# Six TensorE transposes per loop step replaced: a block-wise load with VectorE transposes, and score rows spread through DRAM

## The chip, the cores and the metric

The kernel runs on one core of one Trainium2 chip. The metric is device time in microseconds (us) of a whole execution, as the median of several executions. Engines are named as the profile names them: PE is the matrix engine TensorE, DVE is VectorE, ACT is ScalarE, and SP is the engine whose queue issues all the DMAs here.

## The reference, cut to what matters

Two graph layers over 128 batches of 128 nodes with 512 features. The inputs are `x` (128, 128, 512), `adj` (128, 128, 128) and a mask of ones.

```python
# layer 0, per batch: h = relu(layernorm(x))
Xw = h @ Wv + bv
sj, si = Xw @ aw[:d, 0], Xw @ aw[d:, 0]
e = leaky_relu(sj[:, None, :] + si[:, :, None] + ab[0], 0.2)
alpha = A * exp(e)
transition = alpha / (sum(alpha, axis=-1, keepdims=True) + 1e-12)
for k in range(3):
    H = H + Xk @ Wk[k] + bk[k];  Xk = transition @ Xk
x = x + relu(H)
# layer 1: h = relu(layernorm(x)); q, k = split(h @ Wqk); v = h @ Wv
agg = adj @ (k * mask)
w = inv_scale * mask * sum(q * agg, axis=-1)
x = x + softmax(w, axis=1)[:, :, None] * v
```

Three things in it need something turned by 90 degrees. `sj` is a column with one value per node (partition), and every partition needs all 128 values as a row. The softmax over `w` needs the same for its maximum and its sum. The product `adj @ k` needs A^T: the kernel hands PE the left operand of a product in transposed form.

## The kernel before

The kernel works on pairs of batches (`G` = 2), so it has 64 loop steps. In each step it runs layer 0 of pair p and layer 1 of pair p-1. The scores come from h by two dot products per batch on DVE, with folded weights `u_bc`. The parts that the change and the argument touch:

```python
    def spread(dst, col):                 # a column to a row on every partition
        nc.tensor.transpose(dst, col.to_broadcast([P, P]), ident)

    def norm0(p):
        ...
        h = H[p] = norm_relu(xg[p], "h", front)
        HV[p] = by_blocks(h)              # h to DRAM and back, block-wise
        s = S[p] = small.tile([P, G, 2], FP, name="s")
        for j in range(G):
            for a in range(2):            # the four score sums, DVE
                nc.vector.scalar_tensor_tensor(junk, h[:, j, :], 1.0, u_bc[:, a, :], ...,
                                               accum_out=s[:, j, a:a + 1])

    def attention(p):
        for j in range(G):
            spread(pz[:, j, :], s[:, j, 0:1])                          # PE, 2 transposes
        ... z = pz + s1 + cz, leaky step, exp, times A, row sums, t ...
        for j in range(G):
            nc.tensor.transpose(pa[:, j, :], a[:, j, :], ident)        # PE, 2 transposes: A^T
        ... ACT copies pa into AT[p] with the mask as scale

    def finish(p, yv, w):
        for j in range(G):
            spread(pw[:, j, :], w[:, 0, j:j + 1])                      # PE, 2 transposes
        ... maximum (DVE), exponential (ACT), sum, x = x + weight * v, store

    # the loop: strassen0 is 7 layer-0 products; its steps run between them
    steps = (lambda: (begin(n), attention(n), end()), lambda: t_transposed(n))
    strassen0(p, steps); propagate(p + 1)
    H2[p] = norm_relu(X1[p], ...); hv2 = by_blocks(H2[p])
    yv = strassen1(p - 1); w = aggregate(p - 1, yv)   # layer 1
    prepare0(p + 1); ...; norm0(p + 2)
```

`end()` calls `finish` for the pair whose weights are ready. `strassen0` and `strassen1` accumulate their products in three PSUM banks each, and DVE must read a bank before PE may write the next sum of products into it. `t_transposed` transposes the transition matrix on PE, and ACT copies it out.

## Time and profile before

| of the kernel before | value | how to read it |
|---|---|---|
| time | 2432.89 us (2430.91 to 2434.4, 6 runs) | |
| PE busy | 2382.0 us, 98% of the span | PE has hardly a gap |
| DVE busy / ACT busy | 74% / 27% | both have room on average |
| mean granted PE clock | 0.995 | near full speed; the changed kernel below shows it falling after a wait |
| loop period | 36.70 us | from two equal points of the chain of waits |
| DMAs that write pieces under 64 bytes to DRAM | none | no record stands for the new 4-byte writes |

The prediction shows the lines that carry this. A "period" is the distance in time between two equal points of the chain in successive loop steps. With PE at 98%, the sum of PE's pieces in one period is what a change has to lower.

### The profile page before, as it was taken

The numbers are of one execution on the slowest core, as the hardware profiler recorded it, in microseconds if no ns is written. First come the engines' busy times: TensorE is split into PE (matmuls) and PEld (weight loads), VectorE is DVE, ScalarE is ACT, GpSimd is POOL, SyncE is SP. The second block draws the span as 40 slices with busy tenths as digits, with TensorE's granted clock in tenths as the row PEclk, the third lists the DMA queues.
The fourth block names the chain that finished last, engine by engine and source line by source line (L and its number), as shares of the span: only waits on it lengthen the run. The fifth ranks groups of instructions, "written<-read, shape, count | busy, mean of one in ns | idle before, by whom it ended". The sixth has DMA issues, their size and how long they took to land.

```text
span 2429.0 us, 27235 instructions
## 1 busy us (share of the span) xinstructions
PE 2382.0 (98%) x9289; PEld 1694.0 (70%) x9289; DVE 1791.6 (74%) x4776; ACT 647.6 (27%) x1549; POOL 0.7 (0%) x6
## 2 busy tenths in 40 slices
PE   4999999999999999999999999999999999999997
PEld 3676776776776776776776766766767767767764
DVE  6677777777777777777777777777777777777764
ACT  2223223222222222222222222222232232222221
POOL 0000000000000000000000000000000000000000
PEclk9999999999999999999999999999999999999998
DMA  6233232332332332331332332332332323323311
GB/s 202 72 100 92 80 100 87 85 100 81 91 100 75 97 100 67 105 100 63 109 99 64 108 94 70 102 95 75 100 93 79 100 88 84 100 83 89 96 52 52
DMA packets 236939, 220.49 MB, mean 91 GB/s; under 512 B 14336, under 2 KB 170112, under 8 KB 236800
## 3 DMA queue, kind: packets, MB, share of 16 engines
q1 hardware_dynamic: 236800, 218.75, 31.0%
q8 instruction: 73, 1.20, 0.2%
q14 instruction: 66, 0.54, 0.1%
HBM read 118.03 MB, written 100.66 MB: 90 GB/s over the span
## 4 chain that ended last, share of the span: by engine, by line
PE 97%; DVE 2%; DMA 1%; ACT 0%; issue 0%; SPq 0%; DVEq 0%; ACTq 0%
PE pm L340 79%; PE pt L319 9%; PE pt L411 4%; PE pt L307 1%; PE pt L138 1%; PE pt L303 1%; PE pm L205 1%; PE pt L292 1%; DMA wv_sb<-in_L_gnn_Wv_dram 0%; DVE st L218 0%; DVE junk L249 0%; DVE junk L147 0%; DVE x L378 0%; DVE x L265 0%; DMA hv<-hd 0%
## 5 line engine op out<-in xcount | busy, mean ns | idle before, releaser
L340 PE MATMUL pm<-t,sx 128*128 128x256 f32 x2304 | 518.2, 379 | 0.0
L340 PEld LDWEIGHTS pm<-t,sx 128*128 128x128 f32 x2304 | 432.8, 190 | 56.2
L340 PE MATMUL pm<-b,x 128*128 128x256 f32 x1536 | 362.8, 379 | 0.0
L340 PE MATMUL pm<-f,sx 128*128 128x512 f32 x768 | 344.9, 598 | 0.3 <-DVE s L392 0.2
L340 PEld LDWEIGHTS pm<-b,x 128*128 128x128 f32 x1536 | 282.3, 190 | 60.1 <-issue 30.1
L321 ACT COPY x<-pt 128x512 f32<-128x512 f32 x256 | 148.9, 582 | 500.1 <-PE pt L319 500.1
L340 PEld LDWEIGHTS pm<-f,sx 128*128 128x128 f32 x768 | 141.5, 190 | 194.0 <-issue 154.5
L340 PE MATMUL pm<-e,x 128*128 128x512 f32 x512 | 242.5, 596 | 6.6 <-DVE x L265 6.6
L319 PE MATMUL pt<-tt,h 128*128 128x256 f32 x1024 | 234.5, 383 | 0.9 <-ACT tt L308 0.9
L319 PEld LDWEIGHTS pt<-tt,h 128*128 128x128 f32 x1024 | 196.4, 192 | 28.7 <-ACT tt L308 1.5
L249 DVE SCALAR_TENSOR_TENSOR junk<-h,u_bc 128x512 f32<-128x512 f32 x256 | 176.4, 689 | 8.5 <-ACT h L233 1.8
L340 PE MATMUL pm<-b,sx 128*128 128x256 f32 x768 | 176.2, 379 | 0.0
L340 PE MATMUL pm<-t,x 128*128 128x256 f32 x768 | 176.2, 379 | 0.0
L233 ACT ACTIVATE h<-x,rs 128x512 f32<-128x512 f32 x128 | 97.2, 807 | 289.9 <-PE pt L411 278.3
L265 DVE STREAM_TRANSPOSE x<-hv 128x512 f32<-128x512 f32 x256 | 166.4, 688 | 4.7 <-DMA hv<-hd 3.8
L340 PEld LDWEIGHTS pm<-e,x 128*128 128x128 f32 x512 | 97.7, 191 | 103.1 <-issue 92.2
L340 PEld LDWEIGHTS pm<-b,sx 128*128 128x128 f32 x768 | 145.9, 190 | 19.8
L340 PEld LDWEIGHTS pm<-t,x 128*128 128x128 f32 x768 | 145.9, 190 | 19.8
L400 DVE TENSOR_TENSOR yv<-pm,s 128x512 f32<-128x512 f32 x64 | 44.2, 691 | 128.7 <-PE pm L340 128.7
L233 ACT ACTIVATE h<-xg,rs 128x512 f32<-128x512 f32 x128 | 97.3, 807 | 118.7 <-DVE rs L230 118.7
L411 PE MATMUL pt<-h,aT 128*128 128x512 f32 x256 | 120.5, 592 | 0.5 <-ACT h L233 0.5
L340 PE MATMUL pm<-f,x 128*128 128x512 f32 x256 | 120.3, 592 | 0.0
(102 smaller groups left out, 2508.3 us busy)
## 6 DMA issues: line engine op xcount, KB each, us to landing
hd<-h SPq DMA_DIRECT2D x128, 512.0 KB, 3.3
hv<-hd SPq DMA_DIRECT2D x512, 128.0 KB, 3.3
xg<-in_x_dram SPq DMA_DIRECT2D x64, 512.0 KB, 3.6
out_dram<-x SPq DMA_DIRECT2D x64, 512.0 KB, 3.1
ag<-in_adj_dram SPq DMA_DIRECT2D x64, 128.0 KB, 3.0
b<-in_L_gnn_Wk_dram SPq DMA_DIRECT2D x8, 256.0 KB, 3.4
w<-in_L_gnn_Wqk_dram SPq DMA_DIRECT2D x8, 256.0 KB, 5.3
wv_sb<-in_L_gnn_Wv_dram SPq DMA_DIRECT2D x1, 1024.0 KB, 7.6
```

Source lines behind the costliest of these rows:

```text
L138: nc.tensor.transpose(dst, col.to_broadcast([P, P]), ident)
L205: nc.tensor.matmul(pm[c], wt[0][:, c * P:(c + 1) * P], wt[1], start=(o == 0), stop=(o == DC - 1))
L233: nc.scalar.activation(h[:, j, :], src[:, j, :], AF.Relu, bias=rs[:, 1, j:j + 1], scale=rs[:, 0, j:j + 1])
L249: nc.vector.scalar_tensor_tensor(junk, h[:, j, :], 1.0, u_bc[:, a, :], op0=OP.mult, op1=OP.mult, accum_out=s[:, j, a:a + 1])
L265: nc.vector.transpose(dst[:, j].rearrange("p f (n b) -> p f n b", n=Q), hv[:, j].rearrange("p n (f a) -> p f n a", f=Q))
L292: nc.tensor.transpose(pa[:, j, :], a[:, j, :], ident)
L303: nc.tensor.transpose(pt[:, j, :], t[:, j, :], ident)
L319: nc.tensor.matmul(pt[:, c].rearrange("p k n -> p (k n)"), h[:, j, at:at + P], tt[:, j].rearrange("p k n -> p (k n)"), start=True, stop=True)
L321: nc.scalar.copy(X[p][:, 1:3, j, kh].rearrange("p k c n -> p c k n"), pt)
L340: nc.tensor.matmul(bank[:, :r.shape[-1]], left[i][:, k, c * P:(c + 1) * P], r, start=(first and at == 0), stop=(at == len(chunks) - 1), sk ...
L400: nc.vector.tensor_add(o[0][1], b, s[:, 0])
L411: nc.tensor.matmul(pa, at[:, j, :], h2[:, j, :], start=True, stop=True)
```

## The change

The intent is to take six small PE transposes out of each loop step. A^T is loaded a second time, as 32x32 blocks already in their transposed places (`agb`), and DVE transposes inside the blocks. The score column and the weight column are written to DRAM as 4-byte pieces and read back as one 1 KB row broadcast to all 128 partitions. To give those round trips time, the score sums move forward, between the layer-1 products. The core of the diff:

```diff
+        agb[p] = loads.tile([P, G, Q, S32], FP, name="agb", bufs=2)
+        v = adj[s].rearrange("g (q b) (c i) -> c b (g q) i", b=S32, i=S32)
+        for c in range(Q):
+            nc.sync.dma_start(agb[p][c * S32:(c + 1) * S32].rearrange("p g q i -> p (g q) i"), v[c])
...
+    def spread_pair(col, name, by_dma):
+        if by_dma:
+            d = dram.tile([G, N], FP, name=f"{name}d")
+            nc.sync.dma_start(d.rearrange("g n -> n g"), col)
+            dst = front.tile([P, G, N], FP, name=name, bufs=1)
+            nc.sync.dma_start(dst.rearrange("p g n -> p (g n)"), bcast(d, 0, G * N))
+            return dst
...                                        # attention
-        for j in range(G):
-            spread(pz[:, j, :], s[:, j, 0:1])
...
-        for j in range(G):
-            nc.tensor.transpose(pa[:, j, :], a[:, j, :], ident)
+        nc.vector.transpose(AT[p].rearrange("p g n -> p (g n)"),
+                            agb.pop(p).rearrange("p g q i -> p (g q i)"))
...                                        # strassen1, before its last two product groups
+        if ahead < NP:
+            score_sums(ahead)              # the four sums, then spread_pair(s, "pz", p > 0)
...                                        # the loop
-                steps = (lambda: (begin(n), attention(n), end()), lambda: t_transposed(n))
+                steps = (lambda: (begin(n), attention(n)), lambda: (t_transposed(n), end()))
...
-            ends.append((p - 1, yv, w))
+            ends.append((p - 1, yv, w, spread_pair(w[:, 0], "pw", p < NP)))
```

The set-up code was also reordered (the projection weights are loaded in four pieces, and norm0 of the next pair moves forward). The first scores and the last weights keep their PE transposes.

More of the change, by code (lines that the diff above doesn't have):

```diff
@@ L64, in bcast @@
         return bass.AP(tensor=ap.tensor, offset=ap.offset + offset, ap=[[0, P], [1, n]])
-    xg, ag = {}, {}
+    xg, ag, agb = {}, {}, {}
     def load(p):
@@ L83, with spread @@
     nc.sync.dma_start(aw_bc.rearrange("p a d -> p (a d)"), bcast(aw, 0, 2 * D))
-    wv0_sb = upool.tile([P, DC, D], FP, name="wv0_sb")
-    nc.sync.dma_start(wv0_sb, wv0.rearrange("(c p) o -> p c o", p=P))
+    ident = const.tile([P, P], FP, name="ident")
+    make_identity(nc, ident)
+    eps = const.tile([P, 1], FP, name="eps")
+    nc.vector.memset(eps, EPS)
+    def spread(dst, col):
+        nc.tensor.transpose(dst, col.to_broadcast([P, P]), ident)
+    u_bc = const.tile([P, 2, D], FP, name="u_bc")
+    ucol = setup.tile([P, 2, DC], FP, name="ucol")
+    ccol = setup.tile([P, 2], FP, name="ccol")
+    for c in range(DC):
+        wv0_sb = upool.tile([P, D], FP, name="wv0_sb", bufs=2)
+        nc.sync.dma_start(wv0_sb, wv0[c * P:(c + 1) * P])
+        for a in range(2):
+            junk = front.tile([P, D], FP, name="junk", bufs=1)
+            nc.vector.scalar_tensor_tensor(junk, wv0_sb, 1.0, aw_bc[:, a, :], op0=OP.mult,
+                                           op1=OP.mult, accum_out=ucol[:, a, c:c + 1])
     bv_bc = upool.tile([P, D], FP, name="bv_bc")
@@ L118 @@
         if k:
-            bk_bc.append(setup.tile([P, D], FP, name=f"bk{k}_bc"))
+            bk_bc.append(upool.tile([P, D], FP, name=f"bk{k}_bc"))
         nc.sync.dma_start(bk_bc[k], bcast(bk, k * D, D))
@@ L129 @@
             rows(e[kh, nh][:, :, 1, :], wv1[:, nh * HD:(nh + 1) * HD], kh)
-    ident = const.tile([P, P], FP, name="ident")
-    make_identity(nc, ident)
-    eps = const.tile([P, 1], FP, name="eps")
-    nc.vector.memset(eps, EPS)
-    def spread(dst, col):
-        nc.tensor.transpose(dst, col.to_broadcast([P, P]), ident)
-    u_bc = const.tile([P, 2, D], FP, name="u_bc")
-    ucol = setup.tile([P, 2, DC], FP, name="ucol")
-    ccol = setup.tile([P, 2], FP, name="ccol")
     for a in range(2):
-        for c in range(DC):
-            junk = front.tile([P, D], FP, name="junk", bufs=1)
-            nc.vector.scalar_tensor_tensor(junk, wv0_sb[:, c, :], 1.0, aw_bc[:, a, :],
-                                           op0=OP.mult, op1=OP.mult, accum_out=ucol[:, a, c:c + 1])
         pu = ps_t.tile([P, DC, P], FP, name="pt")
@@ L235, in norm_relu @@
         return h
-    H, HV, S, X, SX, AT, T, TT, X1, H2, X2, SX2 = ({} for _ in range(12))
+    H, HV, S, PZ, X, SX, AT, T, TT, X1, H2, X2, SX2 = ({} for _ in range(13))
     def norm0(p):
@@ L244, in norm0, with score_sums @@
         HV[p] = by_blocks(h)
+    def score_sums(p):
+        h = H[p]
         s = S[p] = small.tile([P, G, 2], FP, name="s")
@@ L250, in norm0 @@
                                                op1=OP.mult, accum_out=s[:, j, a:a + 1])
+        PZ[p] = spread_pair(s[:, :, 0], "pz", p > 0)
     def by_blocks(h):
@@ L266, in transposed, with attention @@
                                 hv[:, j].rearrange("p n (f a) -> p f n a", f=Q))
-    def attention(p):
-        a, s = ag.pop(p), S.pop(p)
+    def spread_pair(col, name, by_dma):
[5 more added lines that the diff above has]
+            return dst
         pz = ps_t.tile([P, DC, P], FP, name="pt")
         for j in range(G):
-            spread(pz[:, j, :], s[:, j, 0:1])
+            spread(pz[:, j, :], col[:, j:j + 1])
+        return pz[:, :G]
+    def attention(p):
+        a, s, pz = ag.pop(p), S.pop(p), PZ.pop(p)
         z = front.tile([P, G, N], FP, name="z", bufs=1)
@@ L277, in attention @@
         nc.vector.scalar_tensor_tensor(z, z, 0.2, z, op0=OP.mult, op1=OP.max)
-        ex = front.tile([P, G, N], FP, name="ex")
+        ex = z
         nc.scalar.activation(ex, z, AF.Exp)
@@ L288, in attention @@
             nc.vector.tensor_scalar(t[:, j, :], ex[:, j, :], d[:, 1, j:j + 1], None, op0=OP.mult)
-        pa = ps_t.tile([P, DC, P], FP, name="pt")
-        for j in range(G):
-            nc.tensor.transpose(pa[:, j, :], a[:, j, :], ident)
         AT[p] = front.tile([P, G, N], FP, name="aT", bufs=3)
+        nc.vector.transpose(AT[p].rearrange("p g n -> p (g n)"),
+                            agb.pop(p).rearrange("p g q i -> p (g q i)"))
         for j in range(G):
             b = p * G + j
-            nc.scalar.activation(AT[p][:, j, :], pa[:, j, :], AF.Copy, scale=maskT[:, b:b + 1])
+            nc.scalar.activation(AT[p][:, j, :], AT[p][:, j, :], AF.Copy, scale=maskT[:, b:b + 1])
     def t_transposed(p):
@@ L379, in strassen0, with strassen1 @@
                                            op0=OP.max, op1=OP.add)
-    def strassen1(p):
+    def strassen1(p, ahead):
         product = products(SX2.pop(p), R1)
@@ L418, in aggregate, with finish @@
         return w
-    def finish(p, yv, w):
-        pw = ps_t.tile([P, DC, P], FP, name="pt")
-        for j in range(G):
-            spread(pw[:, j, :], w[:, 0, j:j + 1])
-        nc.vector.tensor_reduce(w[:, 1], pw[:, :G, :], AX.X, OP.max, negate=True)
+    def finish(p, yv, w, pw):
+        nc.vector.tensor_reduce(w[:, 1], pw, AX.X, OP.max, negate=True)
         for j in range(G):
@@ L445 @@
     norm0(0)
+    score_sums(0)
     begin(0)
@@ L451 @@
     norm0(1)
+    score_sums(1)
     R1 = None
@@ L462 @@
                 n = p + 1
-                steps = (lambda: (begin(n), attention(n), end()), lambda: t_transposed(n))
+                steps = (lambda: (begin(n), attention(n)), lambda: (t_transposed(n), end()))
             else:
-                steps = (end, lambda: None)
+                steps = (lambda: None, end)
             strassen0(p, steps)
@@ L478 @@
             hv2 = by_blocks(H2[p])
+        if p + 2 < NP:
+            norm0(p + 2)
         if p > 0:
-            yv = strassen1(p - 1)
+            yv = strassen1(p - 1, p + 2)
+        elif p + 2 < NP:
+            score_sums(p + 2)
+        if p > 0:
             w = aggregate(p - 1, yv)
@@ L491 @@
             SX2[p] = left_sums(a, late["p"], "sx2", [1, HD])
-        if p + 2 < NP:
-            norm0(p + 2)
     end()
```

## The prediction

> **What bounds the kernel now.** I read, in this order: the summary, the chain that ended last, the same chain inside one step of the loop, the busy time of that step, then the timeline around the operations that the change moves, and last the start and the end. The kernel does 64 pairs of batches; I call the repeating stretch between two equal points of the chain a period.
>
> The chain is TensorE work (PE) nearly from end to end; inside a period (columns: start us, length us, what) it has no piece of another engine:
>
> ```profile
> PE 97%; DVE 2%; DMA 1%; ACT 0%; issue 0%; SPq 0%; DVEq 0%; ACTq 0%
> ...
> 1225.46 5.18 PE pm L340 x24
> 1230.64 0.22 PE pt L138 x2
> 1230.86 0.22 PE pt L292 x2
> 1231.08 0.22 PE pt L138 x2
> 1231.30 5.18 PE pm L340 x24
> 1236.48 0.22 PE pt L303 x2
> ...
> 1262.16 5.18 PE pm L340 x24
> 1267.34 0.22 PE pt L138 x2
> ```
>
> The six transposes that the change removes are the three 0.22 us rows between the 24-record products: two for the score rows (L138), two for the adjacency (L292), two for the layer-1 weights (L138). The period is 1267.34 - 1230.64 = 36.70 us. The busy table of one period (window, its length, then PE, PEld, DVE, ACT, POOL, clock, DMA share, GB/s) says PE is never idle, VectorE (DVE) has 9 us free and the DMA engines 70%:
>
> ```profile
> 1225.50:1262.20 36.70, 36.70 (x145) 26.22 (x144) 27.59 (x74) 10.02 (x25) 0.00 (x0) 1.00 0.30 90
> ```
>
> A busy PE alone would not prove a limit, but the chain's pieces add up: 18.12 us of layer-0 products (84 records at 0.216), 3.45 propagation, 12.08 layer-1 products, 1.72 aggregation, 0.22 + 0.44 for the transition matrix, 0.66 for the six transposes: 36.7.
>
> **What the Trainium skill says.** "TensorE: Matmul & The Clock Gate", Part 4 (PE-mode transpose), gives about 275 ns for a 128x128 transpose in one kernel. The trace agrees on the record (mean 274 to 278 ns) but in the chain two take 0.22 us: records overlap, and what a transpose costs a full PE is 0.11 us. "VectorE: DVE Perf Modes", The three transpose paths, says DVE transposes 32x32 blocks, not a 128x128 tile; hence the block-wise load. Here a 128x512 block transpose (L265) takes 688 ns. "DMA: Bandwidth & Descriptors", Rules for kernel authors, says a DMA that reads what another wrote must be issued only after the first one's completion; the same page's Anatomy of one DMA puts the fixed cost near 2.0 us. So the spread through DRAM costs two latencies in a row. The trace agrees on both: times to landing (last column, us), and the wait of the DMA queue (total, times, longest):
>
> ```profile
> hd<-h SPq DMA_DIRECT2D x128, 512.0 KB, 3.3
> hv<-hd SPq DMA_DIRECT2D x512, 128.0 KB, 3.3
> ...
> e<-in_L_gnn_Wv_dram SPq DMA_DIRECT2D x16, 64.0 KB, 2.0
> ...
> SPq L259 <- DMA hd<-h: 125.5, 66, 2.4
> ```
>
> **Part 1: PE work removed.** In steady state six transposes a period, 6 x 0.11 = 0.66 us; the period should become 36.04 us. The order of the built kernel shows PE otherwise unchanged within a period. Scores and adjacency of pairs 2 to 63 and weights of pairs 0 to 61 lie under a full PE: 62 x 0.66 = 40.9 us. Pairs 0 and 1 are in the start, where PE idles, and the last weights keep their PE transposes.
>
> **Part 2: DVE and ACT.** Added: one 128x256 block transpose, about 0.4 us (half of L265's 688 ns plus overhead, an estimate). Cheaper: z read from SBUF instead of PSUM; z (401 ns each, L276) should approach the SBUF form of L288 (280 ns), saving 0.24, and the maximum (414 ns) a little. Net about zero on DVE's 27.6 us. ACT scales the adjacency from SBUF as it did from PSUM (364 ns). None is on the path.
>
> **Part 3: does the round trip fit?** DVE's order is what can hurt. The score sums (four L249, 0.76 us each with their accumulator reads) move from after the aggregation into the middle of the layer-1 products, where DVE waits for PE. Rows of before (start, length, operation, idle before):
>
> ```profile
> 1217.52 1.52 ACT L233 ACTIVATE h<-xg,rs 128x512 f32<-128x512 f32 x2 [1.91 <-DVE rs L230]
> ...
> 1218.63 0.69 DVE L395 TENSOR_TENSOR s<-pm,s 128x512 f32<-128x512 f32 x1 [1.15 <-PE pm L340]
> ...
> 1222.07 0.69 DVE L400 TENSOR_TENSOR yv<-pm,s 128x512 f32<-128x512 f32 x1 [2.02 <-PE pm L340]
> ...
> 1226.26 0.08 DVE L414 DVE_READ_ACCUMULATOR junk<-pt,wscale,yv 128x1 f32 x1
> ...
> 1230.68 0.42 DVE L363 TENSOR_TENSOR s<-pm,s 128x256 f32<-128x256 f32 x1 [0.85 <-PE pm L340]
> ```
>
> In this clock: h is half ready at 1218.3; the new order is sum, L395, sum, L396, sum, sum, so the fourth sum ends near 1222.65. The 4-byte write to DRAM (256 descriptors; nothing like it stands alone in the trace, I take 2.3 to 2.8 us) lands about 1225.2, the 128 KB broadcast read another 2.5 later: scores at about 1227.7. The DMA engines are idle then. DVE is free at 1226.35, so it loses some 1.4 us, which the moved 3 us of sums pay for. The deadline is L363, now behind the attention on DVE: it frees the bank into which PE's fourth product adds, 3 x 2.59 us after 1225.46, at 1233.2. From the scores to the end of L363 I add z 0.55, block transpose 0.38, leaky step 0.43, two bias adds 0.8, row sums with their wait for the exponential 0.6, normalisation 0.95, L363 0.42: 4.1 us. 1227.7 + 4.1 = 1231.8; margin 1.4 us. The weights' round trip (write about 1226.4, read behind the 1 MB of hd writes) lands about 1232, just where DVE first asks for it, with over 2 us before the next bank is due. A second, thinner place is L395: behind one sum it ends at 1219.7 instead of 1219.3, and PE wants that bank at 1220.3. So no new stall expected, but two margins of 0.6 and 1.4 us.
>
> **Part 4: the start.** In before, PE waits for pair 1's attention before the first layer-0 products; the changed order starts them before it. But they need pair 0's block-wise h:
>
> ```profile
> 34.66 0.39 SPq L255 DMA_DIRECT2D hd<-h  x1
> ...
> 43.30 1.30 DVE L265 STREAM_TRANSPOSE x<-hv 128x512 f32<-128x512 f32 x2 [0.36 <-DMA hv<-hd]
> ...
> 45.70 5.24 PE pt L319 x16
> 50.94 15.55 PE pm L340 x72
> ```
>
> The queue issues in order, about 0.48 us each; ahead of that hd stand 52 DMAs now and 63 then (eight block loads of A, three more pieces of Wv), and the third and fourth pieces wait for DVE. I place the hd at 39.1, its transposes 8.65 later (as now) at 47.75, the first product at 48.4. It then runs cold (L319 took 5.24 us for what later takes 3.45; the granted clock is 0.56 between 40 and 50 us), about 1.7 us lost. Products 18.1, pair 1's transition matrix 0.7 and propagation 3.45, now after the first product instead of before it, end at 72.4 against 68.7: +3.7 us.
>
> **Part 5: the end.** The last-but-one weights come by DMA, behind a 512 KB write, ahead of the last block transposes on DVE: some +0.8 us.
>
> Sum: 2432.9 - 40.9 + 3.7 + 0.8 = 2396.5, about 2396 us, 1.5% less.
>
> **Rivals.** (a) The round trip is late: if the 4-byte write takes 4 us or more instead of 2.5, its margin is gone and every further 0.1 us costs 6 us over 62 periods; 0.5 us of stall takes back three quarters of the gain (2427). For: no such write in the trace, thin margins. Against: idle DMA engines then, only 16 descriptors for each engine. (b) The adjacency's 1024 pieces of 128 bytes a period and twelve more issues crowd the DMA queue, so that h's blocks come late: for: they share one queue; against: DMA share 0.30, and they are issued after the blocks; at most some tens of us. (c) The transposes were hidden: 2433 plus the start's loss; against: the chain and the sum of its pieces leave no room. (d) The start gains: the products begin earlier than I place them; 2386 to 2390.
>
> **Range and chances.** The 40.9 us is firm; the start may be 4 us better or 5 worse; a stall of 0.1 to 0.3 us a period is what can spoil it, so the range leans up: 2387 to 2414. Over 2% faster needs under 2384.3, 8 us more than PE gives: 0.05. Over 2% slower needs stalls of 1.4 us a period: 0.05. Within 2%: 0.90.
>
> **What would show it.** Right: a period of 36.0 us in the chain, PE alone in it, no idle before the fourth layer-0 product, pz landed before 1229 in the clock above, the first layer-0 product near 48.4 us and the transposes of the layer-1 weights (L196 of before) near 72. Wrong: PE waiting for DVE's bank reads (L363 or L395 of before), DVE waiting for pz over 3 us, a 4-byte write landing over 4 us, or the first full product well before 48 us.

## The result

| | before | after |
|---|---|---|
| time, median us (range, runs) | 2432.89 (2430.91 to 2434.4, 6) | 3337.1 (3330.58 to 3338.86, 6) |
| ratio after/before [95%] | | 1.3715 [1.3697, 1.3733] |
| PE busy, share of the span | 98% | 78% |
| mean granted PE clock | 0.995 | 0.887 |
| loop period, us | 36.70 | 51.21 |

A ratio here is the mean time of one kernel's fast runs over the mean of the other's fast runs of the same rounds, so it is not quite the ratio of the medians quoted. The change made the kernel 37% slower, where 1.5% faster was predicted.

The chain that ended last, of the changed kernel (by engine, then by line), is no longer a chain of PE work:

```profile
DMA 49%; PE 42%; DVE 3%; ACT 3%; SPq 1%; issue 1%; DVEq 0%; ACTq 0%
PE pm L359 34%; DMA pwd<-w 21%; DMA pzd<-s 16%; DMA pw<-pwd 8%; PE pt L338 6%; DMA pz<-pzd 3%; PE pt L326 2%; ACT ej L446 1%; DVE junk L258 1%; ACT yv L419 1%; DVE w L443 1%; SPq L284 1%; ACT tt L323 0%; DMA hv<-hd 0%; SPq L120 0%
```

Inside one period the same chain reads (start us, length us, what):

```profile
1673.10 8.75 DMA pzd<-s
1681.86 0.34 SPq L284
...
1682.30 12.72 DMA pwd<-w
...
1695.04 4.81 DMA pw<-pwd
...
1699.87 0.43 DVE w L443
...
1700.33 0.88 ACT ej L446 x4
...
1701.30 0.27 ACT tt L323
...
1724.31 8.34 DMA pzd<-s
```

`pzd<-s` is the score column written to DRAM in 4-byte pieces, and `pwd<-w` is the same for the weights. Each carries 1 KB. They take 8.75 and 12.72 us. The table of DMA issues of the changed kernel says the same over all 63 (the last column is the median us from issue to landing):

```profile
hd<-h SPq DMA_DIRECT2D x128, 512.0 KB, 14.7
...
pz<-pzd SPq DMA_DIRECT2D x63, 128.0 KB, 5.3
pw<-pwd SPq DMA_DIRECT2D x63, 128.0 KB, 4.8
...
pzd<-s SPq DMA_DIRECT2D x63, 1.0 KB, 8.4
pwd<-w SPq DMA_DIRECT2D x63, 1.0 KB, 13.0
```

512 KB written right behind `pwd` (`hd<-h`) lands after 14.7 us, where the same write took 3.3 before. What it does to PE stands in the timeline of that period (start, length, operation, and in brackets the idle time before it with what ended it):

```profile
1686.85 0.60 DVE L296 TENSOR_SCALAR z<-pz,s,cz 128x128 f32<-128x128 f32 x2 [9.10 <-DMA pz<-pzd]
...
1690.69 4.92 PE L359 MATMUL pm<-t,sx 128*128 128x256 f32 x12 [6.05 <-DVE s L382]
...
1701.61 1.13 PE L326 MATMUL pt<-tt,t 128*128 128x128 f32 x4 [4.91 <-ACT tt L323]
```

DVE waits 9.10 us for the scores. Behind the attention in DVE's order stands L382, which reads the PSUM bank that PE's fourth product needs (L363 of the kernel before), and PE waits 6.05 us for it. Later ACT's exponentials of the weights (L446) stand ahead of the copy of the transposed transition matrix (L323) in ACT's order, and PE waits 4.91 us for that copy. Over the whole run the waits of PE are:

```profile
PE pm L359 <- DVE s L382: 432.1, 61, 12.3
...
PE pt L326 <- ACT tt L323: 229.9, 54, 5.7
```

The windows show more about the late DMA (us, then busy PE, PEld, DVE, ACT, POOL, then granted clock, DMA share, GB/s), for the whole period and for the 8.70 us in which only the score write is under way:

```profile
1673.10:1724.31 51.21, 40.25 (x139) 28.27 (x138) 27.60 (x75) 9.95 (x24) 0.00 (x0) 0.90 0.52 72
1673.10:1681.80 8.70, 8.70 (x33) 6.02 (x32) 3.51 (x8) 1.52 (x2) 0.00 (x0) 1.00 0.02 1
```

In the second row the DMA engines are 2% busy and move 1 GB/s. Nothing is in the way of this write; it is the write itself that does not complete. The DMA view of 1673 to 1682 us says where in those 8.75 us the engines are busy (40 slices of 0.225 us, tenths busy; then the records of the SP queue, `q1`):

```profile
DMA  0000420000000000000000000000003000000000
q1 hardware_dynamic: 272, 0.00, 1.6%
```

All 272 records of the queue lie in slices 5 and 6, before 1674.35 (the 3 further on is the one record in this window that is not of `q1`; it belongs to the queue for instructions). The write counts as landed only at 1681.85. So by their records the DMA engines are done with the pieces about 1.2 us after the issue, and the other 7.5 us pass after that. In apart64 below, the same 272 records end about 0.5 us before the landing.

In the first row PE is busy for 40.25 us of 51.21. The 10.96 us of idle time are exactly the two waits above (6.05 + 4.91).

### The profile page after: what moved, and what is told of

It is laid out like the page before. It is cut to its first block, busy times and chain, and to the rows that moved or that the text cites. A ratio compares the mean times of both kernels' runs of the same rounds, so it can differ in the third digit from the quotient of the medians.

```text
span 3335.2 us, 26949 instructions
## 1 busy us (share of the span) xinstructions
PE 2596.7 (78%) x8909; PEld 1818.6 (55%) x8909; DVE 1792.2 (54%) x4840; ACT 643.7 (19%) x1549; POOL 0.7 (0%) x6
## 3 DMA queue, kind: packets, MB, share of 16 engines
q1 hardware_dynamic: 358896, 243.82, 48.4%
## 4 chain that ended last, share of the span: by engine, by line
DMA 49%; PE 42%; DVE 3%; ACT 3%; SPq 1%; issue 1%; DVEq 0%; ACTq 0%
PE pm L359 34%; DMA pwd<-w 21%; DMA pzd<-s 16%; DMA pw<-pwd 8%; PE pt L338 6%; DMA pz<-pzd 3%; PE pt L326 2%; ACT ej L446 1%; DVE junk L258 1%; ACT yv L419 1%; DVE w L443 1%; SPq L284 1%; ACT tt L323 0%; DMA hv<-hd 0%; SPq L120 0%
## 5 line engine op out<-in xcount | busy, mean ns | idle before, releaser
L359 PE MATMUL pm<-t,sx 128*128 128x256 f32 x2304 | 661.6, 453 | 432.1 <-DVE s L382 432.1
L359 PEld LDWEIGHTS pm<-t,sx 128*128 128x128 f32 x2304 | 526.9, 232 | 549.9 <-DVE s L382 456.6
L359 PE MATMUL pm<-b,x 128*128 128x256 f32 x1536 | 432.5, 433 | 19.3 <-DVE x L275 13.6
L359 PEld LDWEIGHTS pm<-b,x 128*128 128x128 f32 x1536 | 332.4, 224 | 97.4 <-issue 29.7
L296 DVE TENSOR_SCALAR z<-pz,s,cz 128x128 f32<-128x128 f32 x126 | 37.9, 343 | 627.6 <-DMA pz<-pzd 627.6
L443 DVE TENSOR_REDUCE w<-pw 128x2 f32<-128x256 f32 x63 | 26.4, 420 | 520.5 <-DMA pw<-pwd 520.5
L326 PE MATMUL pt<-tt,t 128*128 128x128 f32 x256 | 63.9, 392 | 229.9 <-ACT tt L323 229.9
L326 PEld LDWEIGHTS pt<-tt,t 128*128 128x128 f32 x256 | 48.9, 265 | 252.4 <-ACT tt L323 252.0
L446 ACT ACTIVATE ej<-pw,w 128x128 f32<-128x128 f32 x126 | 49.5, 393 | 662.9 <-DVE w L443 662.9
L315 ACT ACTIVATE aT<-aT,maskT 128x128 f32<-128x128 f32 x128 | 44.3, 393 | 644.0 <-DVE aT L311 640.4
## 6 DMA issues: line engine op xcount, KB each, us to landing
hd<-h SPq DMA_DIRECT2D x128, 512.0 KB, 14.7
```

Of the source, the lines that this page charges most:

```text
L296: nc.vector.tensor_scalar(z[:, j, :], pz[:, j, :], s[:, j, 1:2], cz, op0=OP.add, op1=OP.add)
L315: nc.scalar.activation(AT[p][:, j, :], AT[p][:, j, :], AF.Copy, scale=maskT[:, b:b + 1])
L326: nc.tensor.matmul(pt[:, j, :], t[:, j, :], tt[:, j, 0, :], start=True, stop=True)
L359: nc.tensor.matmul(bank[:, :r.shape[-1]], left[i][:, k, c * P:(c + 1) * P], r, start=(first and at == 0), stop=(at == len(chunks) - 1), sk ...
L443: nc.vector.tensor_reduce(w[:, 1], pw, AX.X, OP.max, negate=True)
L446: nc.scalar.activation(ej, pw[:, j, :], AF.Exp, bias=w[:, 1, j:j + 1], accum_out=w[:, 2, j:j + 1])
```

## The experiments

The theory (latency of the write; it is not the "Theory L" in the text of probe_three): a DRAM write of 4-byte pieces side by side completes in 8 to 9 us, the scores and weights come late by that, and everything else follows. Rivals were: the wait comes from the new order of the steps (score sums moved, `end()` late); the second load of A crowds the queue; or the broadcast read is what is slow. Every kernel passed the comparison with the reference.

### a_only: both spreads back on PE, the rest as changed

```diff
-        PZ[p] = spread_pair(s[:, :, 0], "pz", p > 0)
+        PZ[p] = spread_pair(s[:, :, 0], "pz", False)
...
+        def on_pe():                      # the PE transposes, when the consumer asks
+            pz = ps_t.tile([P, DC, P], FP, name="pt")
+            for j in range(G):
+                spread(pz[:, j, :], col[:, j:j + 1])
+            return pz[:, :G]
+        return on_pe
...
-            ends.append((p - 1, yv, w, spread_pair(w[:, 0], "pw", p < NP)))
+            ends.append((p - 1, yv, w, spread_pair(w[:, 0], "pw", False)))
```

> The changed kernel with all three kinds of spread (scores and layer-1 weights) back on PE, at the places where they stood before; the adjacency alone stays on the block-wise load and the DVE transpose. Theory (the 4-byte writes to DRAM are the whole loss): 2433 - 62 x 0.22 us for two transposes a period + 3.7 us at the start = about 2423 us. Rival (the 1024 pieces of 128 bytes and the extra issues crowd the DMA queue): over 2480 us, with h's blocks or the stores landing several us later than 3.3 us.

Measured: 2448.75 us (2446.82 to 2450.12) against 2431.97, ratio 1.0069 [1.0052, 1.0086]. Of the 904 us that the change lost, 888 are gone, so the spreads through DRAM caused them, and neither the load of A (its blocks land 2.7 us after issue) nor the new order did. The expected 2423 was missed by 26 us. The period is 36.98 us, and the chain of the page has turned to VectorE:

```profile
PE 58%; DVE 33%; issue 5%; ACT 2%; DMA 1%; SPq 1%; DVEq 0%; ACTq 0%
```

In the period's chain PE ends the weights' transposes (L95) at 1246.63. The maximum, the exponentials and then DVE's whole list up to L414 at 1262.38 follow with hardly a gap, and PE's layer-1 products wait for L414. In the new order `end()` stands after `t_transposed`, so with the weights on PE the list starts too late. That is a cost of this hybrid, not of the changed kernel, whose chain has no L414 in it.

### pz_dma and pw_dma: one spread by DMA at a time

```diff
# pz_dma
-            ends.append(... spread_pair(w[:, 0], "pw", p < NP))
+            ends.append(... spread_pair(w[:, 0], "pw", False))   # on PE
# pw_dma
-        PZ[p] = spread_pair(s[:, :, 0], "pz", p > 0)
+        PZ[p] = spread_pair(s[:, :, 0], "pz", False)             # on PE
```

> Scores by DMA as in the change, layer-1 weights on PE as before. Theory (each round trip stalls PE on its own): scores come at 1222.65 + 8.4 + 0.1 + 5.0 = 1236.2 in the clock of the prediction, the bank is free 4.1 us later at 1240.3 against 1233.2 wanted, so 7 us of stall in each of 62 periods: about 2840 us. Rival (the loss comes from the two round trips and the writes of h getting in each other's way): under 2600 us.

> Weights by DMA as in the change, scores on PE as before. Theory (each round trip stalls PE on its own; the write lands 8.9 to 13 us after 1226.4 in the clock of the prediction, the read 4.9 later, and PE waits for the copy of the transition matrix, which stands behind the weights' exponentials on ACT and was due at 1236.9): 5 to 9 us a period, 2730 to 2980 us. Rival (only the score trip matters): under 2480 us.

Measured: pz_dma 2865.93 us and pw_dma 2932.4 us, single runs. Against a_only each spread adds 417 and 484 us. The sum, 901, is close to the 888 between a_only and the changed kernel, so the two costs are nearly additive. Both times lie near or inside what was expected (about 2840, and 2730 to 2980). In pw_dma the route was another than expected: PE cannot transpose the transition matrix before DVE has written `t` (L311), which stands behind the maximum that waits for the weights. It does not wait for ACT's copy. That the sum fits although the routes differ is partly luck. The waits of the two traces (first pz_dma, then pw_dma) show different victims:

```profile
DVE z L299 <- DMA pz<-pzd: 484.2, 62, 9.0
```

```profile
PE pt L325 <- DVE t L311: 401.2, 63, 7.6
```

In pz_dma the score write lands after 7.7 us. In pw_dma the weights' write lands after 8.8 us and not 13.0: without the scores' broadcast read queued 0.44 us ahead of it, about 4 us are gone. The `hd` write behind it still takes 11.8 us (5.7 in pz_dma).

### probe_writes, probe_two, probe_three, probe_four: the disputed write by itself

All four are a_only plus DMAs whose result nobody reads, one per pair, issued when the scores are ready (probe_two also at the time of the weights). For example:

```diff
         PZ[p] = spread_pair(s[:, :, 0], "pz", False)
+        probe(p, s, h)
...
+        if k == 0:                         # 4-byte pieces side by side
+            d0 = dram.tile([G, N], FP, name="d0")
+            nc.sync.dma_start(d0.rearrange("g n -> n g"), s[:, :, 0])
+        elif k == 1:                       # the same pieces, 64 bytes apart
+            d1 = dram.tile([G, N, 16], FP, name="d1")
+            nc.sync.dma_start(d1[:, :, 0].rearrange("g n -> n g"), s[:, :, 0])
```

> The kernel of a_only plus one extra DMA a period that nothing reads, issued when the score sums are done; eight forms take turns (about 8 samples each): 256 x 4 bytes into 1 KB of DRAM as in the change; the same with the pieces 64 bytes apart; 512 bytes apart; 128 x 8 bytes into 1 KB; 128 x 64 bytes; 128 x 512 bytes; 256 x 4 bytes into SBUF; 128 x 4 bytes into 512 bytes of DRAM. Theory A (small writes to the same DRAM lines go one after another in the memory, some 33 ns each): contiguous 8 to 9 us, spread by 512 bytes 2 to 3 us, half as many pieces about 5 us, SBUF 2 us. Theory B (each engine pays about 0.5 us for every small piece, wherever it goes in DRAM): spread as slow as contiguous, 8 to 9 us, halves with half the pieces. Theory C (small pieces are slow anywhere): SBUF slow too.

> As probe_writes, other forms (4 samples each). When the score sums are done: 256 x 4 bytes 8, 16 and 32 bytes apart, so that 8, 4 and 2 pieces share 64 bytes; 128 x 8 bytes side by side followed by the 1 KB broadcast read of them; the broadcast read of 1 KB written long ago; a read of 128 different pieces of 1 KB. When the weights are done, just before the 1 MB writes of h: 256 x 4 bytes side by side, and 64 bytes apart. Expected, if pieces that share 64 bytes queue up at some 0.3 to 0.45 us each: 8 bytes apart about 4 us, 16 bytes about 2.5, 32 bytes about 2. If the line that counts is 32 bytes long, 32 bytes apart is already at 1.6 and 8 bytes apart about 3. Broadcast reads 4 to 5 us whether fresh or old, different pieces 2 to 2.5. Before the writes of h: side by side 12 to 13 us and the writes of h then land in 14 us instead of 3.8; 64 bytes apart about 2 us and the writes of h as without it.

> As probe_writes, five more forms (12 samples each): 16, 32 and 64 pieces of 4 bytes side by side (the first 16, 32, 64 partitions), the last 16 partitions, and 128 pieces of 4 bytes 8 bytes apart. Theory L (what counts is how many pieces fall into the same 64 bytes, lines beside each other go on at the same time): 16, 32 and 64 pieces all take about 6 us, like the 6.7 of 128; 128 pieces 8 bytes apart about 2.8. Theory T (all pieces to one small region go one after another): time grows with their number, 16 pieces under 2.2 us, 32 about 2.7, 64 about 4.

> The kernel with A alone (spreads on PE) plus one unread DRAM write per pair at the scores' time, all pieces of 4 bytes from 16 partitions: 32 pieces in two neighbouring runs of 64 bytes; 32 in two runs 1 KB apart; 64 in four neighbouring runs; 64 in four runs 1 KB apart; 64 in four runs 128 bytes apart. The probes so far: 16 pieces in one run of 64 bytes 1.3 us, 32 side by side 3.1, 64 side by side 6.4, 128 side by side 6.6, 256 pieces 16 bytes apart 1.6. Theory B, pieces collide when they share a block larger than 64 bytes: two neighbouring runs 3.1, two far runs 1.3, four neighbouring runs 6.4, four far runs 1.3 to 1.6, four runs 128 bytes apart between those. Theory N, it is the number of pieces that sit beside another piece, wherever their run lies: 3.1, 3.1, 6.4, 6.4, 6.4. Theory P, it takes more than 16 source partitions: all five 1.3 to 1.6. The time is that of A alone, about 2449 us, and says nothing here.

Measured (min / median / max us from issue to landing, each from one trace):

| what is written | layout in DRAM | landing |
|---|---|---|
| 256 pieces of 4 B (as in the change) | side by side, 1 KB | 8.6 / 8.9 / 9.6 |
| 256 x 4 B | 8 B apart | 3.0 / 3.2 / 3.2 |
| 256 x 4 B | 16 B apart | 1.5 / 1.6 / 2.7 |
| 256 x 4 B | 32 B apart | 1.5 / 1.6 / 2.2 |
| 256 x 4 B | 64 B apart | 1.6 / 1.6 / 2.1 |
| 256 x 4 B | 512 B apart | 1.5 / 1.5 / 1.6 |
| 128 x 4 B | side by side, 512 B | 6.5 / 6.7 / 7.4 |
| 128 x 4 B | 8 B apart | 2.6 / 2.8 / 4.1 |
| 64 x 4 B | side by side | 6.1 / 6.4 / 7.0 |
| 32 x 4 B | side by side | 2.9 / 3.1 / 3.2 |
| 16 x 4 B | side by side, 64 B | 1.3 / 1.3 / 1.3 |
| 16 x 4 B, from the last 16 partitions | side by side, 64 B | 1.3 / 1.3 / 1.5 |
| 128 x 8 B | side by side, 1 KB | 2.6 / 2.8 / 3.5 |
| 128 x 64 B | side by side | 1.4 / 1.4 / 1.7 |
| 128 x 512 B | side by side | 1.6 / 1.6 / 1.6 |
| 256 x 4 B | into SBUF in place of DRAM | 1.8 / 1.8 / 2.6 |
| 32 x 4 B from 16 partitions | two neighbouring runs of 64 B | 3.0 / 3.1 / 3.3 |
| 32 x 4 B from 16 partitions | two runs, 1 KB apart | 1.3 / 1.4 / 2.8 |
| 64 x 4 B from 16 partitions | four neighbouring runs | 5.9 / 6.9 / 7.9 |
| 64 x 4 B from 16 partitions | four runs, 128 B apart | 2.3 / 2.6 / 2.9 |
| 64 x 4 B from 16 partitions | four runs, 1 KB apart | 1.3 / 1.4 / 2.4 |

What follows: it is not the size of a piece alone, nor the number of pieces alone, nor DRAM as such. 256 pieces of 4 bytes land in 1.6 us as soon as 16 bytes lie between their starts. Of pieces that lie side by side, the cost comes when one DMA writes several neighbouring runs of 64 bytes (a single piece that fills such a run, 128 x 64 B, took 1.4). It grows from one run (1.3) over two (3.1) to four (6.4 to 6.9), and then little more to eight (6.7) and sixteen (8.9). probe_four's theory B, that pieces collide in a block larger than 64 bytes, came within 0.5 us for each of its five writes, two of whose numbers were taken from earlier probes; the theories of mere count and of partitions are out.

Of the earlier theories most had missed a number: half as many pieces took 6.7 us and not 5 (probe_writes, A), pieces 8, 16 and 32 B apart took 3.2, 1.6 and 1.6 and not 4, 2.5 and 2 (probe_two, 64 bytes), and in probe_three 16 pieces took 1.3 us against theory L's 6, and 64 pieces 6.4 against theory T's 4. The line of 32 bytes of probe_two had its two numbers about right (3.2 and 1.6), but does not explain why 16 pieces in 64 bytes cost nothing.

Inside one run of 64 bytes 16 pieces do not cost anything visible, and why that is so, and which unit makes the neighbours wait, these probes do not settle.

In probe_two the `hd` write landed after 10.6 to 10.9 us behind a side-by-side probe, but after 3.4 to 3.6 behind one with 64 bytes between pieces. The 12 to 13 us expected for the dense write at the weights' time were missed (9.0, which fits pw_dma's 8.8), and so were the 14 us for `hd`. Reads of 1 KB broadcast to 128 partitions took 4.2 us when just written and 3.2 when old; 128 different rows of 1 KB took 2.1. (4 to 5 had been expected, fresh or old.) So the broadcast read is slow too, but by 1 to 2 us and not by 7. Being just written is not what costs: in rows below, the scores' read of a row just written in 128-byte pieces lands after 2.9 us, where the changed kernel's takes 5.3.

### apart64: the changed kernel with the pieces 64 bytes apart

```diff
-            d = dram.tile([G, N], FP, name=f"{name}d")
-            nc.sync.dma_start(d.rearrange("g n -> n g"), col)
+            d = apart[name]                # [G, N, 16], zeroed once at the start
+            nc.sync.dma_start(d[:, :, 0].rearrange("g n -> n g"), col)
```

`apart[name]` is one buffer for the whole run, where the changed kernel takes them in turn. The read is left as it was, so it fetches 1 KB of mostly zeros: the values are wrong. The comparison with the reference passes all the same, so its tolerance does not see these values, and "correct" says little about the spreads in any run here.

> The changed kernel with one thing altered: the 256 four-byte pieces of each score and weight write go to DRAM 64 bytes apart instead of side by side. The read still fetches 1 KB in one piece, so the values are wrong on purpose (16 of 256 are this period's, the rest zeros). Number and size of the pieces, their source, the queue's order and every other instruction stay. Theory (writes to the same 64-byte line go one after another in the memory): the writes land in under 2.5 us, no stall, 2390 to 2400 us plus up to 1 us for the zeroing. Rival (the number of four-byte pieces, or the round trip, is what costs): stays near 3337 us.

Measured: 2392.88 us (2392.01 to 2392.94) against 2432.7, ratio 0.9838 [0.9824, 0.9853]. Only the addresses of two writes changed in the loop, 1 KB per pair each, and 944 us went. In its trace the writes land in 1.6 us (first fence, DMA issues), and PE is busy in the whole period at full clock (second fence, one window):

```profile
pzd<-s SPq DMA_DIRECT2D x63, 1.0 KB, 1.6
pwd<-w SPq DMA_DIRECT2D x63, 1.0 KB, 1.6
```

```profile
1208.71:1244.69 35.98, 35.98 (x140) 25.69 (x139) 27.57 (x76) 10.07 (x24) 0.00 (x0) 1.00 0.39 103
```

This is the decisive run. The order of the steps, the second load of A, the two broadcast reads and the waits of the queue are all still there. One thing follows along: the scores' read lands after 2.9 us in place of 5.3, as it does in rows, where it reads fresh values.

### rows: right values, and long pieces

The column is turned into rows on DVE first (32x32 transposes of a 128x64 tile with the column in it), so the DRAM write has eight pieces of 128 bytes.

```diff
-            nc.sync.dma_start(d.rearrange("g n -> n g"), col)
...
+            r = small.tile([P, G, S32], FP, name=f"{name}r")
+            nc.vector.transpose(r.rearrange("p g i -> p (g i)"), col.rearrange("p g i -> p (g i)"))
+            nc.sync.dma_start(d.rearrange("g (k i) -> k g i", i=S32), r[::S32])
```

> The changed kernel, but the score and weight columns are first turned into rows by a 128x64 block transpose on DVE, so that the write to DRAM is 8 pieces of 128 bytes instead of 256 of 4 bytes; the broadcast read stays. Theory (the 4-byte write is slow, 8.4 and 13 us): the writes land in 2 to 2.5 us and the time falls to between 2395 and 2460 us; the upper part if the broadcast read keeps its 5.0 us, because the scores then come some 1 us a period too late. Rival (a write to DRAM followed by a read is slow as such, whatever its pieces): writes still land in 7 us or more, 2800 us or more.

Measured: 2392.82 us (2391.34 to 2394.51) against 2431.97, ratio 0.9837 [0.9823, 0.9852], PE busy 98%. The expected range, 2395 to 2460, was missed by 2 us on the good side. It beats both kernels. The issues of the SP queue in one period (start, length, what) show that the queue could issue the read 1.59 us after the write:

```profile
1206.88 0.53 SPq L288 DMA_DIRECT2D pzd<-pzr  x1
1208.47 0.34 SPq L290 DMA_DIRECT2D pz<-pzd  x1
```

The extra transposes cost DVE 0.20 to 0.25 us each, off the path. The built program also issues `hd` before the weights' write (1209.78 and 1210.79), so rows changes a little more than the write; the run that changes it alone is apart64.

### pairs: 8-byte pieces

```diff
-            d = dram.tile([G, N], FP, name=f"{name}d")
-            nc.sync.dma_start(d.rearrange("g n -> n g"), col)
+            d = dram.tile([N, G], FP, name=f"{name}d")     # both batches of a node side by side
+            nc.sync.dma_start(d, col)
...
```

> The changed kernel with the two batches' scores (and weights) of a partition kept side by side, in the source and in DRAM: 128 pieces of 8 bytes instead of 256 of 4 bytes, still one dense 1 KB, same queue order. In the probes this write landed in 2.8 us and the read of it in 4.2. Theory: issued at 1221.7 in the clock of the prediction (the third sum, not the fourth, releases it), the scores come at 1221.7 + 2.8 + 4.6 = 1229.1, which is just the latest time that the prediction worked out, so a stall of 0 to 0.3 us a period: 2393 to 2412 us. Rival (the many small pieces as such, or writing before reading, cost several us): over 2450 us.

Measured: 2471.74 us (2466.92 to 2476.27) against 2432.58, ratio 1.0162 [1.0148, 1.0176]. The expectation (2393 to 2412) was missed, and the number lies where the rival had put it (over 2450). But the rival's cause is not what the trace shows: the score write lands after 2.9 us as the probe had it. It is the weights' write that comes late, after 4.9 us (probe: 2.8). PE is idle for 0.65 and 1.45 us in two successive periods:

```profile
1201.82:1238.72 36.90, 36.25 (x139) 25.61 (x139) 27.40 (x75) 9.96 (x24) 0.00 (x0) 1.00 0.46 100
1238.72:1276.42 37.70, 36.25 (x140) 25.62 (x139) 27.40 (x75) 9.96 (x24) 0.00 (x0) 1.00 0.45 98
```

Both idle times end with ACT's copy of the transposed transition matrix, behind the exponentials: the second victim of the changed kernel, now alone. In the second of these periods the weights' write is issued at 1241.34 and the weights are there at 1251.56, 10.2 us later. In apart64 the same takes 7.2 to 7.6 us in two periods. The scores' broadcast read is issued 1.74 us before the weights' write in pairs, with 4.1 us to land, so the two overlap; in apart64 it is issued 3.10 us before and takes about as long, 3.1 us, to land. My reading is that a score write that is only 1.3 us longer pushes the read into the weights' write. No run isolates that, so it is argued and not shown. What can be said of the weights' margin is that a trip of 7.6 us costs nothing, one of 9.4 us (the first of these periods) costs 0.65 and one of 10.2 costs 1.45.

### adj_before: the kernel before, with only A's part of the change

```diff
# in the kernel before
-            nc.tensor.transpose(pa[:, j, :], a[:, j, :], ident)
+        nc.vector.transpose(AT[p].rearrange("p g n -> p (g n)"),
+                            agb.pop(p).rearrange("p g q i -> p (g q i)"))
```

(Two small memory moves of the change come along: `ex = z`, and another pool for `bk_bc`.)

> The kernel before with only the adjacency changed (block-wise load, DVE transpose, no PE transposes of A); nothing else moved. Two PE transposes a period less: 2433 - 62 x 0.22 = 2419 us, plus 1 to 3 us for eight more DMA issues at the start. If instead 2440 or more, as in a_only, the loads of A themselves disturb the steady state; then the wait would be on the DMA of A's blocks.

Measured: 2426.75 us (2426.43 to 2427.23) against 2432.7, ratio 0.9979 [0.9962, 0.9996], just clear of 1. Two transposes off PE are worth 6 us, where about twice that was expected. The period is 36.62 us and not 36.48: the 28 layer-1 products take 12.21 us in the chain where they took 12.08. That is also a gain, but a small one; most of what rows wins (39 us) must come, by difference, from the four spreads and the order that goes with them.

### rows_start: rows, with sixteen set-up loads moved back

```diff
-            rows(e[kh, nh][:, :, 1, :], wv1[:, nh * HD:(nh + 1) * HD], kh)
+    def load_wv1(): ...                    # called after score_sums(1)
```

> The kernel rows with the sixteen loads of the second layer's Wv moved behind the first two pairs' set-up, so that the first hd is not queued behind them. In the trace of after these loads hold the queue from 30.6 to 39.4 us. Theory (the start waits for the first block-wise h, and so for the queue): the first product starts up to 8.8 us earlier than 48.5, and 3 to 8 us of it arrive at the end: 2385 to 2390 us against 2392.8. Rival (the loads are only pushed to where the layer-1 score matrix waits for the queue): 2392 us or more.

Measured: 2387.95 us (2386.83 to 2388.38, 5 rounds) against 2432.58, ratio 0.9818 [0.9804, 0.9831], as expected. The first layer-0 product starts at 41.54 us instead of 49.35 in rows, and the second pair's at 86.17 instead of 92.34. This is the fastest version found. (rows and rows_start ran on different chips; the kernel before took 2431.97 and 2432.58 us there.)

## Why the prediction was wrong

**The step that failed** is in Part 3: "The 4-byte write to DRAM (256 descriptors; nothing like it stands alone in the trace, I take 2.3 to 2.8 us)". It took 8.75 us in the period shown, and 8.4 in the median. The same step hides in "The weights' round trip (write about 1226.4, read behind the 1 MB of hd writes) lands about 1232": that write took 12.72 us. The mechanism was stated rightly and its main term was too small by a factor of three or more.

**The size follows from the prediction's own sum.** It allowed 5.05 us from the fourth sum to the scores. The trace has 13.75 us from the issue to DVE's start on them (1673.10 to 1686.85), 8.7 more: 6.2 of them are the write's (8.76 against 2.55) and 2.5 the read's (4.99 against 2.5). So the read was mis-sized too; behind a write that lands in 1.6 us (apart64, rows) it took 2.9. The issue comes 0.95 us earlier than placed (the write needs only the sums of the first kind, so it goes after the third sum), and 1.4 us were margin: 8.7 - 0.95 - 1.4 = 6.35 us of expected stall, and PE waited 6.05. The second wait, 4.91 us, has the same source, but by a route that the prediction did not name. It looked for the next PSUM bank. What was late was ACT, whose exponentials stand before the copy of the transition matrix.

**The third term is the clock.** PE's work of one period took 40.25 us instead of the 35.98 of apart64, 4.27 more. The Trainium skill, "TensorE: Matmul & The Clock Gate", Part 1: The HAM clock gate, says that PE drops to half its clock after about 3.4 us without work. The trace agrees: PE rested from 1684.64, the granted clock was still 1.00 between 1686.6 and 1687.6 and was 0.50 between 1688.2 and 1690.7. After the 6.05 us of idle time the twelve products took 4.92 us where they take 2.6, and the clock between 1686.8 and 1695.0 was 0.58. After the second wait it was 0.50 again (1703 to 1705). Together 6.05 + 4.91 + 4.27 = 15.23 us per period, which is the whole difference of the periods (51.21 - 35.98). Times 62 that makes 944 us, and the medians of the changed kernel and of apart64 differ by 944.2. That it fits to the last us is luck: one period was taken, and the issues of `pzd` (47.8 to 3199.5 us) are 50.8 us apart in the mean over 62 steps.

**Part 1 was right.** It predicted a period of 36.04 us once the six transposes are gone. apart64 and rows have 35.98 and 35.99, with PE alone in it.

**Part 2 was right in its total.** DVE's work per period stayed at 27.6 us. The block transpose took 0.44 us (predicted 0.4). z from SBUF took 343 ns (hoped: towards 280), the maximum gained nothing (420 ns, 414 before), and ACT's scaling of A took 393 ns and not 364.

**Part 3's second thin place, L395, held.** No wait for it shows in the chain of the changed kernel or of apart64.

**Part 4 was nearly right.** The `hd` was placed at 39.1 us and came at 39.48, its transposes at 47.75 (47.80), the first product at 48.4 (48.56). (How 39.1 was reached is not shown; 34.66 and eleven more issues of 0.48 us make 39.9.) The loss was predicted at 3.7 us; the second layer-0 start is 4.8 us later in rows and 5.4 later in apart64 than in the kernel before. Part 5, +0.8 us at the end, was not tested on its own. The sum of the parts, 2396, stands against 2392.9 (apart64) and 2392.8 (rows): with a short write it would have been right to 4 us. There is some luck in that: the loop gained more than was predicted (0.72 us a period and not 0.66) and the start lost more.

**The rivals and the chances.** Rival (a) named the very mechanism, and its arithmetic is about right: every 0.1 us beyond the margin costs 6 us (without the clock's share). But it went no further than 4 us, and what it listed against itself ("idle DMA engines then, only 16 descriptors for each engine") was no evidence: the engines were indeed idle, at 2%, while the write took 8.7 us. A duration with no record in the trace, which enters 62 times with 1.4 us to spare, does not allow a chance of 0.05 for "slower". Rivals (b) and (c) are out: the blocks of A land in time in a_only, and the transposes' time was really won in apart64. The start of (d) was had only by moving loads (rows_start).

**What stays open.** Which unit delays neighbouring 4-byte writes (the packet records say only that the time passes after the DMA engines have handled them), and why one run of 64 bytes is free of it. Why pairs' weight write takes 4.9 us is argued only. That the changed kernel's 13.0 us are 9 of its own and about 4 from the read ahead of it follows from pw_dma (8.8) and probe_two (9.0), where that read is missing, but no run put the read alone in front of it.

## What to carry to other kernels

A column that goes to DRAM as 4-byte pieces side by side took 8 to 9 us here with nothing ahead of it and 13.0 behind a read, and the same column with 16 bytes or more between the pieces took 1.6: give small pieces room, or turn the column into rows on VectorE first. Where a new kind of transfer stands in every step of a full loop, measure it alone by a probe whose result nobody reads before believing a margin of 1 or 2 us. A stall of PE costs more than its length once the clock falls (4.27 us on top of 10.96 here), and the queue of ACT or DVE that PE depends on is to be read for what stands ahead of the awaited instruction.

## What the Trainium skill lacked or had wrong

- "DMA: Bandwidth & Descriptors", Specifications, says that below 512 B a transfer does a read-modify-write, and Anatomy of one DMA puts the fixed cost near 2.0 us for DMAs that GpSimd issues (here SP issues them). It has nothing on small pieces that lie side by side: 256 pieces of 4 B took 8.9 us side by side, 3.2 at 8 B apart and 1.6 at 16 B or more apart; 128 pieces of 64 B, also under 512 B, took 1.4.
- The same page has no figure for how long such a write holds up what is queued behind it: 512 KB landed after 10.6 to 10.9 us behind it and after 3.4 to 3.6 behind a write with 64 B between the pieces.
- The same page has no figure for a broadcast read: 1 KB read by all 128 partitions took 4.2 us when just written in 8-byte pieces, 2.9 when just written in 128-byte pieces (rows) and 3.2 when old, against 2.1 for 128 different rows.
- "TensorE: Matmul & The Clock Gate", Part 4, gives about 275 ns for a bf16 transpose in one kernel. Here the records of f32 transposes last 274 to 278 ns too, but in a full PE the period fell by 0.72 us for six of them (36.70 to 35.98), at most 0.12 us each.
